# Steps that fill PSUM banks for VectorE go to the front of a cell, and four pairs' first scores are made side by side

## The chip, the cores and the metric

The kernel runs on one core of a Trainium2 chip. The metric is the device time of one execution in microseconds (us). Three runs of the kernel before took 1527.48, 1527.50 and 1529.93 us; the median is 1527.5 us. The core's engines are TensorE (PE: matrix products, results to PSUM), VectorE (DVE), ScalarE (ACT), GpSimd (POOL) and SyncE (SP, which here only issues DMA transfers). PSUM has eight banks of 128 x 512 float32 each; TensorE writes them, VectorE and ScalarE empty them.

## The reference

Two transformer blocks over `x` of 2 sequences x 1024 rows x 256 features, with a context of 2 x 64 rows; everything is float32, with 16 heads of 16 features.

```python
# block 0
q = ln(x);  x = x + mha(q, q)                       # self-attention, 16 heads
x = x + mha(ln(x), ln(ctx))                         # cross-attention over 64 rows
h = ln(x);  logits = h @ router.T                   # 8 experts, the best 2 of each row
x = x + sum over 2 experts of gate * (gelu(h @ fc1.T) @ fc2.T)
# block 1
x = x + self_attention(ln0(x))
x = x + cross_attention(ln1(x), ctx, mask)          # a masked context row gets -10000
x = x + gelu(ln2(x) @ fc1.T + b1) @ fc2.T + b2
```

In each attention `softmax(q k / 4) v` is computed; the largest score of a row is subtracted before the exponential.

## The kernel before

The text calls reference block 0 "block 1" and reference block 1 "block 2", as the change's title does; in the code they are `layer` 0 and 1.

**Cells.** Self-attention of one block is 128 cells in a written-out order (`self_attention`, the loop over `cell`). A cell belongs to one group of four heads, one half of the queries and one 128-key chunk: `h, n = divmod(cell, 8)`. It does two things on TensorE, in four lanes on four row groups (`scores`, L969): "b" tiles, the scores of this cell with keys on the partitions and the row's largest score subtracted, and "a" tiles, the scores of the cell `LEAD` = 10 further on with queries on the partitions. ScalarE empties a "b" bank with an exponential (L947); VectorE empties an "a" bank with a maximum along the row (L937). Every eighth cell `collect(h)` joins the maxima of a group (L1002 to L1004, three VectorE operations; the middle one writes to a PSUM bank out of the free list), and one cell later `largest(h)` transposes them (L835). From cell 118 on there are no "a" tiles.

Exponentials are multiplied with the values in `product` (L1024): either two cells in one PSUM bank, or one cell alone (`alone`) when the cell has little other work. ScalarE copies the result out (L1036), and GpSimd, or VectorE from cell 118 on (`helper()`), adds it up (L1037).

**Other chains in the cells.** Everything else is a `Task`: a generator whose steps give their cost in planned microseconds, or a negative number for a pause. In each cell `Stream.steady(cell, 1.1)` takes one step of each "light" task in order of `rank` while less than 1.1 planned us are spent; `Stream.step` fills odd cells with heavier ones; what is left over decides whether a product is done alone. After the last cell `Stream.rest` runs what remains, by rank and pause. Since the engines' orders are written out this way, each engine executes in exactly the order in which the steps are called.

For each quarter n of the rows, a block has these chains: `cnorm` n (layer norm; statistics L398/L399, roots L381 to L389, centring L412, transposes L424), `asked` n (queries, L1295), `weighed` n (cross-attention weights), `cross` n (division and output projection, L492/L500). Block 1 also has `dispatch` n (rank 70: router, choice of two experts, places, L1568 to L1676, with eight indirect DMA writes from GpSimd), `found` (places of the expert tiles, L1693 to L1802) and the expert slots (`turn` L1926, `first` L1961, `second` L1992). Block 2 ends with the dense layer (`forward`, L2145 and L2157).

**`weighed`** (rank 30) has its own first scores: `scores(g, n, ...)` makes the products of head pairs r = 2n and 2n + 1 of half g (L1337), in block 2 after a product that adds the mask (L1324), and VectorE reduces each bank (L1345). `parts` (L1358/L1359) writes the maxima where `largest` transposes them (L1364); then come `weights` (L1374, L1380, exponential L1385), the products with the values (L1434 and the sums L1444) and the division (L1453, L1459, L1466). In the cells with "a" tiles one step does half of the rows of two pairs; in the later cells and in the rest one step does all rows of two pairs, so four steps make the first scores of a quarter.

PSUM banks are handed out by `bank()` from the front of a list and go back to its end when the step that empties them is written down. A matmul waits for the engine that last emptied its bank.

Of the kernel before, what the change touches and what calls it, by code (L numbers as in the profile page):

```python
# [134 lines left out]
class Task:  # L135

    def __init__(self, steps, cost, first=-99, last=None, mark=None, after=(), rank=0, light=False):
        self.steps, self.left, self.first, self.light = steps, cost, first, light  # L140
        self.soft, self.last = last is None, 9999 if last is None else last
        self.mark, self.after, self.rank = mark, after, rank


class Stream:
# [29 lines left out]
    def steady(self, cell, most):  # L175

        spent = 0.0
        for t in sorted((t for t in self.tasks if t.light), key=lambda t: -t.rank):
            if spent < most and t.first <= cell and self.made.issuperset(t.after):
                spent += max(0.0, self.advance(t, cell) or 0.0)  # L180
        return spent

# [53 lines left out]
def two_blocks(  # L236
# [27 lines left out]
    def bank():  # L264


        i = free.pop(0)
        return i, banks[:, i, :]
# [312 lines left out]
    def self_attention(layer, tail, heads, arrive, extra, when_ready, beside=None):  # L581
# [41 lines left out]
        QB, mx = {}, {}  # L623
# [488 lines left out]
        if layer == 0:  # L1112

            fill_up(-LEAD, 4.0)
            owed = 0.0
            for ahead in range(0, LEAD, 2):
                cell = now[0] = ahead - LEAD
                for n, _ in enumerate(early(ahead)):
                    for go in later.pop(cell + n, []):
                        go()  # L1120
                    if (ahead, n) == (6, 1):
                        collect(0)
                    owed += 1.6
                    while owed > 0.6 and (cost := stream.step(cell)):
                        owed -= cost
                    if (ahead, n) == (8, 0):
                        stream.add(largest(0), 0.75, mark=("QB", 0))
                        stream.until(("QB", 0))
        owed = 0.0
        for cell in range(ncell + 2):  # L1130
            now[0] = cell
            ahead = cell + LEAD
            if ahead < ncell and ahead % 16 == 0:
                need_heads(ahead // 8)
            has_a, has_b = ahead < ncell, cell < ncell
            maxima[0] = has_a
            lanes = []
            for j in range(4):
                tiles = [("b", cell, j)] * has_b + [("a", ahead, j)] * has_a
                lanes.append(tiles[::-1] if j > 1 else tiles)  # L1140
            scores(lanes)
            if ahead % 8 == 7 and has_a:
                h = ahead // 8
                collect(h)
                stream.add(
                    largest(h), 0.75, first=cell + 1, last=cell + 2, mark=("QB", h), rank=99, light=True
                )
            if (cell + 1) % 8 == 0 and cell + 1 < ncell:
                stream.until(("QB", (cell + 1) // 8))
            for go in later.pop(cell, []):  # L1150
                go()
            if cell >= 2 and cell % 2 == 0:
                product([c for c in (cell - 2, cell - 1) if c not in alone])
            if has_a:
                most = 2.2 - stream.steady(cell, 1.1)
                while cell % 2 == 1 and most > 0.9:
                    cost = stream.step(cell, heavy=True)
                    if cost is None:
                        break
                    most -= cost  # L1160
            else:
                owed = min(owed, 3.0) + max(stream.pace(cell), 2.0)
                if cell % 2 == 0 and owed < 2.5:
                    continue
                most = 2.2
                while owed > 0.5 and most > 0.0:
                    cost = stream.step(cell)
                    if cost is None:
                        break
                    owed -= cost  # L1170
                    most -= cost

            if cell % 2 == 1 and most > 1.2 and cell < ncell:
                alone.add(cell - 1)
                product([cell - 1])
# [79 lines left out]
    def cross_tasks(stream, layer, n, pool, first):  # L1255


        att = 2 * layer + 1
        w = weights[att]
        b, t0 = n // 2, 4 * n  # L1260
        name = f"c{layer}{n}"
        held = {}

        def norm():
            xT = held["xT"] = pool.tile([P, 2, 512], F32, tag="cx", name=f"xT_{name}")
            yield from norm_task(t0, 4, "cq" if layer == 0 else "ln1", xT, name)
            if layer == 0:
                add_bias(t0, 4, bias_out[1])

        before = [(m, n - 1) for m in ("cross", "asked")] if n > 0 else ["context"]  # L1270
        stream.add(norm(), 2.0, mark=("cnorm", n), after=before[1:], first=first,
            rank=67 if layer == 0 else 40, light=True)
        stream.add(
            ask(layer, pool, w, name, held), 3.44, mark=("asked", n),
            after=[("cnorm", n), before[0]], rank=30,
        )
        stream.add(
            weigh(layer, b, pool, w, name, held), 13.5,
            mark=("weighed", n), after=[("asked", n)], rank=30, light=True,
        )  # L1280
        stream.add(
            share(w, name, t0, held), 5.0, mark=("cross", n),
            after=[("weighed", n)], rank=50,
        )
# [23 lines left out]
    def weigh(layer, b, pool, w, name, held):  # L1308
# [7 lines left out]
        mx = pool.tile([P, 2, 4, 4, 2], F32, tag="mxc", name=f"mx_{name}")  # L1316
        turned_mx = []

        def scores(g, n, t0=0, nt=4):

            got = [(r, *bank()) for r in (2 * n, 2 * n + 1)]
            for r, _, p in got if layer == 1 else ():
                at = slice(32 * r, 32 * r + 1)
                nc.tensor.matmul(  # L1324
# [146 lines left out]
        if whole:  # L1471
# [2 lines left out]
            cells = [[] for _ in range(22)]  # L1474
            for k in range(8):
                g, n, half = k // 4, k // 2 % 2, k % 2
                cells[k].append((scores, g, n, 2 * half, 2))
                if k % 4 == 3:
                    cells[k].append((parts, g))
            cells[9].append((largest,))  # L1480
# [16 lines left out]
            return  # L1497
        costs = {scores: 1.0 + extra, largest: 0.9, weights: 1.2, undivided: 1.9, division: 0.55}
        rs = range(4)
        for step, *args, wait in (  # L1500
            (scores, 0, 0, None),
            (scores, 0, 1, None),
            (parts, 0, None),
            (scores, 1, 0, None),
            (scores, 1, 1, None),
            (parts, 1, -1.8),
            (largest, -0.8),
            (weights, 0, rs, -1.6),
            (undivided, 0, None),
            (weights, 1, rs, -1.6),  # L1510
            (division, 0, None),
            (undivided, 1, None),
        ):
            step(*args)
            if step in costs:
                yield costs[step]
            if wait:
                yield wait
# [988 lines left out]
```

## Time and profile before

| | |
|---|---|
| median of three runs | 1527.5 us |
| profiled execution, whole | 1523.92 us |
| its span (first to last instruction) | 1522.0 us |
| TensorE busy | 1439.3 us (95%) |
| VectorE busy | 982.7 us (65%) |
| ScalarE busy | 919.9 us (60%) |
| GpSimd busy | 355.3 us (23%) |
| mean granted TensorE clock | 0.986 |
| L937, row maxima on VectorE | 1024 of 683 ns |
| L947, exponentials on ScalarE | 1024 of 603 ns |
| L1345, reductions of the cross scores on VectorE | 96 of 506 ns |
| L1036, copies of products | 145 of 601 ns |
| activation-table loads | 17 |

The cells of block 1 lie between about 65 and 545 us of the span, the rest of block 1 and the expert slots between 545 and 900 us, the cells of block 2 between 900 and 1372 us, and its rest after that. An ordinary cell takes 2.7 us with a product alone and 3.6 us with a pair or with a heavier step. How to read the rows shown further on: a row of waits gives the engine that waited, who released it, the sum, the number and the longest wait; a row of a timeline gives start, duration, engine, line, operation, output and inputs, and in brackets the idle time before it; a row of a stretch gives busy time (and instructions) of PE, PEld (weight loads), DVE, ACT and POOL, the granted clock, the share of the DMA engines and GB/s.

### The profile page before, as it was taken

Reading aid. Unit: us, or ns where it says so; the run is one execution under the profiler, and the core shown is the slowest. Engines: PE = TensorE matmul, PEld = TensorE weight load, DVE = VectorE, ACT = ScalarE, POOL = GpSimd, SP = SyncE. Lnnn points to the kernel's source line nnn. Section 1 sums busy time; section 2 is a strip of 40 time slices with the busy share of each in tenths; the row PEclk is TensorE's granted clock in tenths of the full one; section 3 lists DMA queues with packets and bytes.
Section 4 is the critical chain, followed back from the end, with each engine's and each line's share of the span. In section 5 each row is a group of like instructions: output and inputs, shape, how many; then the busy total and the mean of one; then the engine's idle time right before and its main releaser. Section 6 shows DMA issues by size and latency. Waiting matters only on the chain. (4 is left out here: it accounts for less than half of the span.)

```text
span 1522.0 us, 29849 instructions
## 1 busy us (share of the span) xinstructions
PE 1439.3 (95%) x11172; PEld 830.1 (55%) x11172; DVE 982.7 (65%) x2216; ACT 919.9 (60%) x1797; POOL 355.3 (23%) x488
## 2 busy tenths in 40 slices
PE   6999999999999977999999999999999999999998
PEld 3444444444434445788888664444454454446676
DVE  7867788869778665531115758877886886944210
ACT  3377788777777845323323347877877777783411
POOL 2221234225243122031112023211332322411010
PEclk9899999999999998999999999999999999999999
DMA  8653122111110030666566541132211112000000
GB/s 318 248 217 136 52 70 64 43 47 42 36 51 31 15 115 29 215 240 232 188 203 231 169 150 62 61 108 71 64 50 52 44 36 97 29 10 29 8 14 28
DMA packets 69157, 148.71 MB, mean 98 GB/s; under 512 B 12842, under 2 KB 26668, under 8 KB 68620
## 3 DMA queue, kind: packets, MB, share of 16 engines
q1 hardware_dynamic: 65788, 137.86, 26.6%
q0 software_dynamic: 3216, 8.85, 1.6%
q8 instruction: 91, 1.49, 0.4%
q14 instruction: 62, 0.51, 0.1%
HBM read 94.32 MB, written 51.99 MB: 96 GB/s over the span
## 5 line engine op out<-in xcount | busy, mean ns | idle before, releaser
L937 DVE TENSOR_REDUCE mx_s<-banks 128x1 f32<-128x512 f32 x1024 | 635.4, 683 | 131.2 <-PE banks L969 123.4
L947 ACT ACTIVATE pt_s<-banks 128x512 f32<-128x512 f32 x1024 | 535.2, 603 | 125.9 <-PE banks L969 120.1
L1024 PE MATMUL banks<-pt_s,v_s 128*18 128x512 f32 x2048 | 260.6, 603 | 9.6 <-ACT pt_s L947 5.4
L1037 POOL TENSOR_TENSOR acc_s<-acc_s,part_s 128x512 f32<-128x512 f32 x130 | 166.8, 1283 | 419.5 <-ACT part_s L1036 418.8
L969 PE MATMUL banks<-qb_s,ones 2*128 2x512 f32 x1024 | 200.6, 395 | 0.0
L1992 PE MATMUL banks<-w_slot,h_s 128*128 128x256 f32 x560 | 125.1, 380 | 0.4 <-DVE spread L1004 0.4
L1036 ACT COPY part_s<-banks 128x512 f32<-128x512 f32 x145 | 87.1, 601 | 48.0 <-PE banks L1024 42.6
L1992 PEld LDWEIGHTS banks<-w_slot,h_s 128*128 128x128 f32 x560 | 105.4, 190 | 15.6 <-DVE spread L1004 0.8
L1024 PEld LDWEIGHTS banks<-pt_s,v_s 128*18 128x18 f32 x2048 | 43.5, 97 | 126.8 <-ACT pt_s L947 66.4
L2001 DVE SCALAR_TENSOR_TENSOR ys<-banks,gate,b 128x256 f32<-128x256 f32 x35 | 16.9, 483 | 133.2 <-PE banks L1992 133.2
L969 PEld LDWEIGHTS banks<-qb_s,ones 2*128 2x128 f32 x1024 | 96.6, 186 | 8.9
L1967 ACT ACTIVATE h_s<-banks,w_slot 128x256 f32<-128x256 f32 (+1 forms) x104 | 41.1, 446 | 86.1 <-issue 48.3
L2007 POOL DMA_INDIRECT results<-ys,to x35 | 33.8, 966 | 224.3 <-DVE ys L2001 175.6
L1961 PE MATMUL banks<-xsT,w_slot 128*128 128x256 f32 (+1 forms) x416 | 84.9, 357 | 0.9 <-ACT xsT L431 0.9
L1961 PEld LDWEIGHTS banks<-xsT,w_slot 128*128 128x128 f32 x416 | 70.9, 190 | 12.0 <-issue 2.8
L2145 PE MATMUL banks<-hT_f,w_ff 128*128 128x512 f32 x128 | 57.0, 595 | 0.0
L2157 PE MATMUL banks<-w_ff,h_f 128*128 128x256 f32 x256 | 56.6, 379 | 0.0
L1345 DVE TENSOR_REDUCE mx_c<-banks 128x4 f32<-128x256 f32 (+1 forms) x96 | 44.2, 506 | 17.8 <-PE banks L1337 16.7
L698 PE MATMUL banks<-xT_s,w_att 128*128 128x512 f32 x104 | 50.9, 613 | 3.2 <-ACT pt_s L947 2.4
L1967 ACT ACTIVATE h_s<-banks,spare 128x256 f32<-128x256 f32 (+1 forms) x56 | 21.7, 444 | 51.1 <-PE banks L1961 34.9
L2157 PEld LDWEIGHTS banks<-w_ff,h_f 128*128 128x128 f32 x256 | 48.2, 190 | 7.2 <-issue 1.0
L2148 ACT ACTIVATE h_f<-banks,w_ff 128x512 f32<-128x512 f32 x32 | 21.9, 687 | 48.6 <-PE banks L2145 48.6
(376 smaller groups left out, 2926.8 us busy)
## 6 DMA issues: line engine op xcount, KB each, us to landing
w_slot<-in_ff_w_dram SPq DMA_DIRECT2D x40, 576.0 KB
sorted_rows<-fill SPq DMA_DIRECT2D x36, 520.0 KB
w_slot<-in_ff_w_dram SPq DMA_DIRECT2D x26, 514.0 KB
whole<-acc_s SPq DMA_DIRECT2D x30, 256.0 KB
spare<-in_ff_w_dram SPq DMA_DIRECT2D x14, 514.0 KB
q_parts<-spare SPq DMA_DIRECT2D x13, 512.0 KB
KS<-k_parts SPq DMA_DIRECT2D x12, 512.0 KB
k_parts<-spare SPq DMA_DIRECT2D x10, 512.0 KB
```

Source lines behind the costliest of these rows:

```text
L698: nc.tensor.matmul(p, lhsT=w[:, at + k * D + pair * P : at + k * D + (pair + 1) * P], rhs=xT[b][:, k, blk * 512 : (blk + 1) * 512], start= ...
L937: nc.vector.tensor_reduce(to, sc, AX.X, ALU.max)
L947: nc.scalar.activation(pt, sc, AF.Exp, scale=SCALE)
L969: nc.tensor.matmul(sc, lhsT=lhsT, rhs=rhs, start=now[0] == 1, stop=last)
L1024: nc.tensor.matmul(o[32 * j : 32 * j + VW, :], lhsT=V[b][:, cell % 8, 4 * g + j, :], rhs=exps.pop((cell, j)), start=(cell == cells[0]), st ...
L1036: nc.scalar.copy(part, o)
L1037: helper().tensor_tensor(acc[h], acc[h], part, ALU.add)
L1961: nc.tensor.matmul(ph[:, n, :], lhsT=w[:, at : at + P], rhs=xT[:, k, :], start=(k == 0), stop=(k == 1),)
L1967: nc.scalar.activation(h1[:, f, :rows], ph[:, n, :], AF.Gelu, bias=w[:, W_B1 + f : W_B1 + f + 1])
L1992: nc.tensor.matmul(py, lhsT=h1[:, f, h * P : (h + 1) * P], rhs=w[:, f * D : (f + 1) * D], start=(f == 0), stop=(f == 7),)
L2145: nc.tensor.matmul(ph, lhsT=w1[:, at : at + P], rhs=hT[:, k, :], start=(k == 0), stop=(k == 1))
L2157: nc.tensor.matmul(py[:, n, :], lhsT=h1[:, f, t * P : (t + 1) * P], rhs=w2[:, f * D : (f + 1) * D], start=(f == 0), stop=(f == 7),)
```

## The change

1. A `Task` gets a flag `drains`. The tasks `largest` (QB) and `weighed` have it. In `steady` the tasks with the flag come first whatever their rank, and tasks without it may begin while 1.8 planned us are spent instead of 1.1.
2. `collect(h)` is called after `steady` instead of before it.
3. In block 2's late cells and rest, `scores` takes all four pairs of a half in one step (planned cost 1.7 instead of twice 1.2). Block 1 keeps two pairs a step there.

```diff
-    def __init__(self, steps, cost, first=-99, last=None, mark=None, after=(), rank=0, light=False):
+    def __init__(
+        self, steps, cost, first=-99, last=None, mark=None, after=(), rank=0, light=False, drains=False
+    ):
+        self.drains = drains
...
-        for t in sorted((t for t in self.tasks if t.light), key=lambda t: -t.rank):
-            if spent < most and t.first <= cell and self.made.issuperset(t.after):
+        for t in sorted((t for t in self.tasks if t.light), key=lambda t: (-t.drains, -t.rank)):
+            if spent < most + 0.7 * (not t.drains) and t.first <= cell and self.made.issuperset(t.after):
...
                 h = ahead // 8
-                collect(h)
                 stream.add(
-                    largest(h), 0.75, first=cell + 1, last=cell + 2, mark=("QB", h), rank=99, light=True
+                    largest(h), 0.75, first=cell + 1, last=cell + 2, mark=("QB", h), rank=99,
+                    light=True, drains=True,
                 )
...
                 most = 2.2 - stream.steady(cell, 1.1)
+                if ahead % 8 == 7:
+                    collect(ahead // 8)
...
             weigh(layer, b, pool, w, name, held), 13.5,
-            mark=("weighed", n), after=[("asked", n)], rank=30, light=True,
+            mark=("weighed", n), after=[("asked", n)], rank=30, light=True, drains=True,
...
-        def scores(g, n, t0=0, nt=4):
+        def scores(g, rs, t0=0, nt=4):
 
-            got = [(r, *bank()) for r in (2 * n, 2 * n + 1)]
+            got = [(r, *bank()) for r in rs]
...
-                cells[k].append((scores, g, n, 2 * half, 2))
+                cells[k].append((scores, g, (2 * n, 2 * n + 1), 2 * half, 2))
...
         rs = range(4)
+        if layer == 1:
+            costs[scores] = 1.7
+            halves = [rs]
+        else:
+            halves = [(0, 1), (2, 3)]
         for step, *args, wait in (
-            (scores, 0, 0, None),
-            (scores, 0, 1, None),
+            *((scores, 0, half, None) for half in halves),
             (parts, 0, None),
-            (scores, 1, 0, None),
-            (scores, 1, 1, None),
+            *((scores, 1, half, None) for half in halves),
             (parts, 1, -1.8),
```

In the order of instructions this gives the following. In block 1, TensorE's order is the same up to cell 88 and again from the fourth expert slot's transposes on. In between, the second quarter's `weighed` steps start one cell earlier and stand ahead of the `dispatch` steps of the same cell; `dispatch` of the second quarter begins two cells earlier and has its places by the end of the cells, and its 14 root operations are on GpSimd instead of VectorE. The program has five L1036 copies fewer (more products are done in pairs) and two activation-table loads fewer; all products and all DMA transfers are the same in number. In block 2 TensorE's order is the same up to cell 118; there VectorE's three `collect` operations move back, behind the reductions or statistics of the same cell. From cell 119 to cell 124 the third quarter's `weighed` steps are fewer and come earlier; in the rest only the four score steps of the last quarter become two.

More of the change, by code (lines that the diff above doesn't have):

```diff
@@ L1126, in self_attention @@
                     if (ahead, n) == (8, 0):
-                        stream.add(largest(0), 0.75, mark=("QB", 0))
+                        stream.add(largest(0), 0.75, mark=("QB", 0), drains=True)
                         stream.until(("QB", 0))
```

## The prediction

> **What bounds the kernel now.** Four views carry it, read in this order. First the page: TensorE is busy for most of the span, so a gain has to come out of its waits and out of the slices in which its clock is cut.
>
> ```profile
> span 1522.0 us, 29849 instructions
> PE 1439.3 (95%) x11172; PEld 830.1 (55%) x11172; DVE 982.7 (65%) x2216; ACT 919.9 (60%) x1797; POOL 355.3 (23%) x488
> ```
>
> Second, the waits of TensorE between 390 and 660 us, the only stretch in which its order of work differs much between the two kernels (cell 89 of block 1 to the third expert slot):
>
> ```profile
> PE banks L424 <- DVE xn_c L412: 9.3, 1, 9.3
> PE banks L969 <- DVE mx_c L1345: 3.7, 3, 1.7
> ...
> PE banks L1364 <- DVE spread L1359: 2.3, 1, 2.3
> ```
>
> The second row is what the change is aimed at: scores of a cell (L969) waiting for PSUM banks that VectorE's cross-attention reductions (L1345) empty. Third, busy time by stretch (columns after the width: PE, PEld, DVE, ACT, POOL, granted clock, DMA):
>
> ```profile
> 404.80:427.20 22.40, 17.80 (x178) 9.11 (x176) 21.84 (x54) 13.34 (x26) 6.39 (x5) 0.97 0.11 37
> ...
> 505.80:541.90 36.10, 34.09 (x340) 16.91 (x340) 16.56 (x53) 30.04 (x61) 0.43 (x1) 1.00 0.00 1
> ...
> 563.20:572.60 9.40, 0.05 (x2) 0.05 (x1) 8.20 (x45) 0.84 (x4) 0.00 (x0) 0.63 0.49 192
> ...
> 1242.30:1259.30 17.00, 16.75 (x185) 8.60 (x186) 15.22 (x32) 14.10 (x28) 5.17 (x4) 1.00 0.14 49
> ...
> 425.80:432.60 6.80, 6.80 (x41) 2.44 (x40) 5.31 (x15) 3.94 (x8) 0.00 (x0) 0.50 0.22 72
> ```
>
> VectorE is full in the first row, with TensorE at 17.8 of 22.4 us; TensorE's own waits there come to 4.6 us. Row 4 is the same cells, 93 to 97, in block 2, where no dispatch work is threaded in: they took 17.0 us there, and 24.7 us in block 1 (406.1 to 430.8). The last row is a slice at half clock right behind the full stretch. Fourth, the order of time inside it:
>
> ```profile
> 418.43 1.09 DVE L1609 TENSOR_TENSOR hot_m<-desc,first_m 128x32 f32<-128x32 f32 x1
> 419.44 0.74 DVE L1345 TENSOR_REDUCE mx_c<-banks 128x4 f32<-128x256 f32 x2
> 419.90 0.50 PE L969 MATMUL banks<-QS00h,KS 32*128 32x512 f32 x1 [1.66 <-DVE mx_c L1345]
> ```
>
> The dispatch operations stand ahead of the reduction that frees the bank, and TensorE stops for 1.66 us. One of them takes 1.09 us where its neighbours take 0.19, with a GpSimd addition (1.26 us from 418.20) under way.
>
> **The change part by part.** Costs are against the profiled execution: 1522.0 us of span and 1.9 around it, 1523.9 us in all, 3.6 under the median of 1527.5.
>
> *1. Block 1, cells 89 to 104.* The built order shows weighed.1 (second quarter's cross weights) starting in cell 89, not 90, and keeping that lead; five L1036 copies in all disappear, because more products are done in pairs. One pair of reductions leaves the full stretch for cell 89, where VectorE has room: two at 0.33 us (spacing of the 0.74 us pairs), 0.7 us, certain. Reordering within a full engine gives nothing by itself: 20 score reductions (12.4 us), ten L1345 (3.7 us) and 5.7 us of other work have to be done in any order. The gain above 0.7 lies in what is not full: the wait in cell 89 (0.5 us), and the half clock. In those 6.8 us TensorE lost up to half, 3.4 us. Bounds: a gain of 3.4 if the slice does not come, nothing if it does, a loss of 3.4 if two come; I take a gain of 1.7, half way, since the waits before it get shorter by the one pair but do not go. Sum -2.4 (+2.7 to -5.4, the latter by taking for each of the 16 cells the longer of its TensorE and VectorE work, which leaves 65.6 us where today the same work takes 71.0).
>
> The row says that the clock fell with waits of 1.66 us at the longest. The Trainium skill, "TensorE: Matmul & The Clock Gate", section "What's actually happening", has the clock cut after an idle window of about 3.4 us, which no wait here reaches; by that rule the cut is not of these waits' making, my 1.7 us would be no gain, and the total -3.4.
>
> *2. Block 1, cells 117 to 128.* The ten product steps become six: 4 copies of 0.6 us, 2.4 us off ScalarE, which is at 30.0 of 36.1 us and makes TensorE wait 1.6 us there (L947, L431). I take -1.0, nearer the waits than the copies (-2.4, and on the other side +2.0 by what follows). dispatch.1 comes two cells earlier; its 14 root operations go from VectorE to GpSimd, where the same 14 took 3.9 us (485.2 to 489.1), read three cells later. Cover: three cells of about 3.5 us. If that cover is gone, L1568 on VectorE, and the L1345 reductions queued behind it, wait some 2 us, and TensorE for their banks.
>
> *3. The rest between the blocks.* The longest wait is this one:
>
> ```profile
> 561.48 0.18 DVE L1776 TENSOR_SCALAR row<-row,begin 128x1 f32<-128x1 f32 x1
> ...
> 562.15 0.68 DVE L500 TENSOR_TENSOR x_sb<-x_sb,banks 128x512 f32<-128x512 f32 x1
> ...
> 563.82 0.14 DVE L1799 TENSOR_SCALAR ntu<-ntu 128x16 f32<-128x16 f32 x1
> ...
> 572.56 1.11 PE L424 MATMUL banks<-ident,xn_c 128*128 128x128 f32 x4 [9.35 <-DVE xn_c L412]
> 573.46 1.06 PE L1926 MATMUL banks<-ident,xs 128*128 128x128 f32 x4
> ```
>
> Behind the last projection VectorE adds, measures, takes roots, twice, before TensorE has anything. Eight operations of found.2 (four from 561.48, four from 563.82) sit in that chain; now they precede the last addition: -1.3 us. The L1641/L1642 waits (0.44 and 0.30) leave this stretch: -0.7. The four L1926 transposes now stand ahead of the L424 ones and run inside the wait (their rows' load was issued at 565.4 and DMA is quiet from 569): -0.6; what is queued behind that load's wait is only L424, not ready before. Against it, seven slot.0 operations (2.4 us) now precede xd_m on VectorE; but first matmuls of the slot start 5.9 us after the first L424 today, and the same VectorE work lies before them afterwards. Eight dispatch.1 sends of 1.27 us on GpSimd start some 5 us earlier and delay nothing; SP's list of loads is the same. Two activation-table loads (1.28 us each) fewer on ScalarE, off the path: 0. Sum -2.6; I take -2.0 (+2.4, if the slot's operations are in nobody's shadow, to -4.5, with the half clock that lies from 566 to 576 us cut short).
>
> From the slots on (about 655 us) the orders agree again and TensorE is over 99% busy, so what is gained before arrives at the end.
>
> *4. The three maxima operations moved back in both blocks.* For heads 8, 9, 12, 13 their scratch bank is no longer last in the free list but third last (fifth, once). Nearest row: L969 waiting 0.2 us for L1004. Eight times 0 to 0.2: +0.3 (0 to +1.6).
>
> *5. Block 2's end.* Scores of four pairs in one step:
>
> ```profile
> 1415.79 0.50 PE L1324 MATMUL banks<-mask_f,ones 1*128 1x512 f32 x2
> ...
> 1416.58 0.50 PE L1324 MATMUL banks<-mask_f,ones 1*128 1x512 f32 x2
> ...
> 1422.79 0.19 DVE L1359 TENSOR_TENSOR spread<-mx_c,spread 128x32 f32<-128x32 f32 x1
> 1423.04 0.66 PE L1364 MATMUL banks<-ident,spread 128*128 128x128 f32 x4
> ```
>
> Two pairs cost 0.79 us now, four steps 3.2. Side by side the saving is between 0 and half. In the rest (weighed.3) it is worth nothing: TensorE reaches L1364 as VectorE's eight reductions end, and would wait for what it saves. In cells 119 to 121 the same eight reductions get less cover: from the second step to the transposes lies only one cell's scores (0.8 us) against 0.3 + 4 x 0.6 + 0.4 = 3.1 us, a wait of 2.3 us. Today the corresponding waits are for banks (12.7 us from 1339.6 for some 10.6 us of work, 2.1 lost). Then L1434 comes a cell after the weights, not two, and waits about 1 us; everything is a cell ahead by then. 0 (+3.3 to -2).
>
> Total -2.4 - 1.0 - 2.0 + 0.3 + 0 = -5.1: the profiled execution would take 1518.8 us, the median 1522.4.
>
> **The rivals.** *A, VectorE bound, nothing more:* only 0.7 + 0.8 (parts 1 and 3) come. For it: 21.84 of 22.40 us busy. Against: part 3 is a chain, not throughput. 1526.0. *B, slower:* the wait ahead of L1364 in block 2's cell 121. 2.3 + 1.0 us, and, as the waits above were followed by half clock, a slice of 6.8 us at half: 3.4. +6.7, on top of A's -1.5: 1532.7. It decides once that wait exceeds block 1's gain. Against: bank waits of the same size are there today. *C, both clock slices go:* -5.4 - 1.0 - 4.5 = -10.9, 1516.6. For it: all waits in part 1 lie just before the cut. Against: the cut's phase is not the kernel's.
>
> **How the numbers follow.** Main case 0.50, A 0.19, B 0.18, C 0.13. One measurement of this kernel can tell about 0.2%, 3.1 us, from none: below 1524.4 is faster, above 1530.6 slower. Nine in ten of the main case (0.45) and C (0.13) are faster: 0.58. Most of A (0.17) and some of the main case (0.04) are the same: 0.21. B and the ends of A and of the main case (0.03) are slower: 0.21. The main case's own range is 1518 to 1526. Leaving out the far half of C and what lies beyond B's price gives 1515.5 to 1533.
>
> **What would show it.** Right: L969 waits for L1345 in cells 93 to 97 under 2 us, VectorE still full there but for one cell less; no half clock near 420 to 432; the wait of L424 for xn_c at 8 us or less, with L1926 inside it; block 2 up to cell 118 unchanged within 1 us. Wrong: a new L1364 wait over 3 us in block 2, or part 4's bank waits of more than 0.2 us a head, or a wait of L1568 on GpSimd's roots.

## The result, and the profile after

The changed kernel took 1536.83 us (median; 1534.70 to 1540.53), the kernel before 1527.5 us beside it: a ratio of 1.006, with a 95% interval from 1.0043 to 1.0077. The change costs 9.3 us where the prediction had a gain of 5.1.

The head of the page of the changed kernel:

```profile
span 1534.2 us, 29842 instructions
PE 1442.0 (94%) x11172; PEld 833.0 (54%) x11172; DVE 972.5 (63%) x2199; ACT 916.9 (60%) x1790; POOL 356.8 (23%) x500
```

The work of the five engines is all but the same; the span is 12.2 us longer than in the profile of before (the medians differ by 9.3; a later paragraph says why the two profiles are no clean pair). (Lines moved with the edit: L969 is now L972, L1024 is L1027, L1345 is L1350, L1364 is L1369, L1926 is L1934, L424 is L427, the sends L1676 are L1684.)

The waits of TensorE between 400 and 470 us, the cells 89 to 107 of block 1:

```profile
PE banks L972 <- DVE mx_s L940: 1.4, 1, 1.4
PE banks L1379 <- issue: 1.2, 1, 1.2
...
PE banks L972 <- DVE mx_c L1350: 0.2, 1, 0.2
```

What the change was to remove is gone: scores waiting for the cross reductions fell from 3.7 us to 0.2 (last row). New is a wait for "issue", which means that nothing in the trace explains why TensorE stood still. The same view between 540 and 665 us, the rest between the blocks:

```profile
PE banks L427 <- DVE xn_c L415: 5.6, 1, 5.6
...
PE banks L1934 <- DMA xs<-sorted_rows: 2.3, 1, 2.3
...
PE banks L889 <- issue: 2.2, 4, 1.0
```

The expected order is there too (the L1934 transposes run inside the long wait, which is 5.65 us after them), and again there are stops for "issue", at L889. The order of time around them, with PE, POOL, DVE and ACT rows (the POOL rows are the fifth and the eighth of the eight sends):

```profile
550.07 1.58 PE L1449 MATMUL banks<-pt_c,picks 128*32 128x128 f32 x32
...
551.12 0.97 POOL L1684 DMA_INDIRECT sorted_rows<-xd_m,at_m  x1 [0.17 <-issue]
...
552.26 1.08 PE L883 MATMUL banks<-acc_s,picks 128*64 128x512 f32 x4
...
553.27 0.42 PE L889 MATMUL banks<-acc_s,picks 128*32 128x128 f32 x4
...
554.93 0.96 POOL L1684 DMA_INDIRECT sorted_rows<-xd_m,at_m  x1 [0.30 <-issue]
...
557.14 0.96 DVE L1458 RECIPROCAL inv_c<-banks 128x128 f32<-128x128 f32 x1 [6.62 <-remote]
557.27 0.59 ACT L898 COPY ot_s<-banks 128x512 f32<-128x512 f32 x1 [5.42 <-remote]
```

VectorE's reciprocal needs only the L1449 sums, which TensorE had done at 551.65; ScalarE's copy needs L883, done at 553.34. Both start 1.25 to 1.4 us after GpSimd's last send has ended, within 0.13 us of each other. The trace also keeps the moments at which TensorE raises its semaphore: one at 551.24, the next at 557.12, although four matmuls that raise it had ended from 551.65 on; the four rises then come together, from 557.12 to 557.25. So TensorE's completions reached the others up to 5.5 us late (by the ends that the trace gives for matmuls, which are modelled). Its own matmuls came in small groups meanwhile. TensorE's clock paid a second time (columns: width, PE, PEld, DVE, ACT, POOL, granted clock, DMA share, GB/s):

```profile
551.25:557.15 5.90, 3.39 (x25) 1.35 (x26) 0.01 (x1) 0.59 (x1) 3.73 (x4) 1.00 0.61 224
557.50:567.70 10.20, 8.87 (x34) 8.02 (x35) 5.49 (x25) 2.44 (x6) 0.00 (x0) 0.50 0.00 1
```

VectorE did next to nothing in the first row, and the second is half clock. The same happened at 441 to 448 us, where the sends of dispatch.0 run. Of the ten rises that matmuls ending from 442.03 to 447.35 us call for, the trace has four, so the engines that wait tell it better:

```profile
442.94 0.72 PE L972 MATMUL banks<-KS,QS01l 32*128 32x512 f32 x2
...
447.71 1.29 DVE L940 TENSOR_REDUCE mx_s<-banks 128x1 f32<-128x512 f32 x2 [2.91 <-PE banks L1385]
```

VectorE's third and fourth maximum of the cell need these matmuls, the first of which ended at 443.44. VectorE was free from 444.79 and started at 447.71, 4.3 us after that end; the releaser that the view names, L1385, writes other banks. ScalarE's third exponential started 4.2 us late. Cell 100 takes 8.70 us, and the slice from 444.8 to 455.0 us is at half clock.

Set beside the first profile of before by stretches (cells by the mean start of their four exponentials; us, and differences from before; e-numbers are the experiments below, letters their chips):

| stretch | before | changed | e18: sorting alone, A | e17: maxima alone, A | e9: changed, C | e14: sorting alone, D | e16: before, D |
|---|---|---|---|---|---|---|---|
| to block 1, cell 0 | 65.2 | +0.5 | -1.7 | -1.9 | -1.7 | -2.9 | -1.4 |
| cells 0 to 89 | 325.1 | -0.5 | -0.1 | +1.2 | -1.0 | -0.1 | -1.1 |
| cells 89 to 98 | 40.5 | -2.7 | -2.7 | -1.0 | -3.0 | -4.1 | -2.1 |
| cells 98 to 105 | 28.6 | **+9.1** | **+10.3** | -0.3 | +0.7 | +0.7 | -0.7 |
| cells 105 to 127 | 83.1 | -4.0 | -4.5 | -0.1 | -4.0 | -4.5 | -0.1 |
| rest, to block 2 | 357.2 | **+9.8** | **+7.8** | **+6.5** | -0.4 | -0.4 | +1.2 |
| block 2, 0 to 118 | 435.8 | 0.0 | 0.0 | -0.2 | -0.2 | -1.5 | -0.2 |
| 118 to the end | 186.5 | 0.0 | -0.2 | 0.0 | +1.5 | -0.2 | 0.0 |
| span | 1522.0 | +12.2 | +8.7 | +4.3 | -8.1 | -13.0 | -4.5 |

The whole loss lies in two stretches, and in both GpSimd issues sends. One execution differs from the next by some microseconds (e9 and e14 lie 5.4 and 4.3 us under the medians of their own runs), so the table tells where, and the medians below tell how much.

The two profiles of the first comparison are no clean pair. The profile of before took 1523.9 us, less than each of the five executions that give the median (1526.67 to 1529.93), and it is none of them; it has no late completion and lacks no record of VectorE's semaphore (2051 rises for 2049 instructions), where the profile of the changed kernel lacks 30 (1981 for 2011). The experiments below find the first picture on three chips and the second on one.

### The profile page after: what moved, and what is told of

It reads as the page before. It is cut to its first block, busy times and chain, and to the rows that moved or that the text cites. A ratio compares the mean times of both kernels' runs of the same rounds, so it can differ in the third digit from the quotient of the medians.

```text
span 1534.2 us, 29842 instructions
## 1 busy us (share of the span) xinstructions
PE 1442.0 (94%) x11172; PEld 833.0 (54%) x11172; DVE 972.5 (63%) x2199; ACT 916.9 (60%) x1790; POOL 356.8 (23%) x500
## 5 line engine op out<-in xcount | busy, mean ns | idle before, releaser
L1027 PE MATMUL banks<-pt_s,v_s 128*18 128x512 f32 x2048 | 258.5, 605 | 10.6 <-ACT pt_s L950 5.4
L972 PE MATMUL banks<-qb_s,ones 2*128 2x512 f32 x1024 | 200.5, 395 | 0.0
L1027 PEld LDWEIGHTS banks<-pt_s,v_s 128*18 128x18 f32 x2048 | 43.7, 97 | 130.2 <-ACT pt_s L950 65.3
L1039 ACT COPY part_s<-banks 128x512 f32<-128x512 f32 x140 | 83.9, 599 | 47.4 <-PE banks L1027 43.9
L972 PEld LDWEIGHTS banks<-qb_s,ones 2*128 2x128 f32 x1024 | 96.0, 186 | 8.8
L1975 ACT ACTIVATE h_s<-banks,w_slot 128x256 f32<-128x256 f32 (+1 forms) x104 | 41.1, 446 | 83.1 <-issue 49.2
L1350 DVE TENSOR_REDUCE mx_c<-banks 128x4 f32<-128x256 f32 (+1 forms) x96 | 44.0, 504 | 22.6 <-PE banks L1342 21.3
```

Source lines behind the costliest of these rows:

```text
L972: nc.tensor.matmul(sc, lhsT=lhsT, rhs=rhs, start=now[0] == 1, stop=last)
L1027: nc.tensor.matmul(o[32 * j : 32 * j + VW, :], lhsT=V[b][:, cell % 8, 4 * g + j, :], rhs=exps.pop((cell, j)), start=(cell == cells[0]), st ...
L1039: nc.scalar.copy(part, o)
L1975: nc.scalar.activation(h1[:, f, :rows], ph[:, n, :], AF.Gelu, bias=w[:, W_B1 + f : W_B1 + f + 1])
```

## The experiments

The experiments ran on four chips, here called A (e1 to e4, e17, e18), B (e5 to e8), C (e9 to e12) and D (e13 to e16). Ratios are to the kernel before on the same chip at the same time. Edits are shown by what they come to; in most of these kernels the parts of the change stand behind switches. No profile of the unedited kernel before was taken on A; e2 and e17 have its order in block 1.

| run | kernel | chip | median us | before | ratio, 95% interval | completions late? |
|---|---|---|---|---|---|---|
| e1 | changed | A | 1535.24 | 1526.58 | 1.0047 (1.0032 to 1.0062) | up to 4.7 us |
| e9 | changed | C | 1521.33 | 1521.38 | 1.0004 (0.9992 to 1.0015) | no |
| e13 | changed | D | 1522.95 | 1521.16 | 1.0014 (1.0004 to 1.0023) | no |
| e2 | block 2 only | A | 1529.42 | 1526.58 | 1.0023 (1.0007 to 1.0040) | up to 3.5 |
| e3 | maxima in front | A | 1530.36 | 1526.58 | 1.0020 (1.0010 to 1.0030) | up to 5.4 |
| e4 | no allowance | A | 1532.98 | 1526.58 | 1.0041 (1.0027 to 1.0055) | up to 5.8 |
| e6 | side by side alone | B | 1523.44 | 1521.10 | 1.0016 (1.0004 to 1.0027) | no |
| e17 | maxima moved alone | A | 1530.29 | 1528.02 | 1.0021 (1.0006 to 1.0035) | up to 3.5 |
| e7 | sorting alone | B | 1514.96 | 1521.10 | 0.9958 (0.9941 to 0.9974) | no |
| e10 | sorting alone | C | 1517.38 | 1521.38 | 0.9964 (0.9950 to 0.9979) | no |
| e14 | sorting alone | D | 1515.22 | 1521.16 | 0.9967 (0.9954 to 0.9979) | no |
| e18 | sorting alone | A | 1528.46 | 1528.02 | 1.0010 (0.9995 to 1.0026) | up to 5.8 |
| e8 | sorting, no allowance | B | 1516.24 | 1521.10 | 0.9973 (0.9960 to 0.9986) | no |
| e11 | sorting, no allowance | C | 1514.55 | 1521.38 | 0.9957 (0.9944 to 0.9971) | no |
| e15 | sorting, no allowance | D | 1512.80 | 1521.16 | 0.9951 (0.9936 to 0.9966) | no |
| e5, e12, e16 | before, one execution each | B, C, D | 1522.56, 1523.55, 1519.43 | | | no |

"Late" is the largest distance between the end of a TensorE matmul and the rise of its semaphore inside a gap of over 1.2 us between such rises, taken up to 615 us. In e8 and e10 the records show 1.3 and 1.1 us once, but there rises are missing: in e8 the reciprocal that waits starts at 597.49 us, 0.1 us after its matmul's end. The starts of waiting engines confirm the others: while sends run in the cells, maxima and exponentials begin up to 1.4 us (e2, e4, e17) or 3.6 to 4.3 us (the others) after their matmul's end though the engine is free; in the twelve other profiles never more than 0.9 us. The gaps behind 615 us also fall into sends, and none of the conclusions rests on them. Profiles with late completions, and the chip that has them, are called disturbed, the others clean or undisturbed.

### First on A: which half, which part

e1 is the changed kernel, unedited.

> The changed kernel as it is, profiled a second time. Theory O (the order of block 1 costs the time): cell 100 of block 1 again takes over 8 us, TensorE again stands still for some 4 us while GpSimd sends the rows of dispatch.1 (551 to 557 us in the first profile), each with a half-clock slice behind it, and the span is 1534 us within 3. Theory X (the two stalls belong to that one execution): at least one of them is absent or lies elsewhere, and the span is 5 us or more shorter where it is absent.

The second profile repeats the first: cell 100 takes 8.39 us, completions are late by 4.7 us from 551.45 to 556.58, the rest is 6.8 us longer than before's, the span 1533.9 us. Not the accident of one execution.

e2 keeps block 1 as before. Its edit against the changed kernel:

```diff
+        stream.drain = layer in (1,)
...
-        for t in sorted((t for t in self.tasks if t.light), key=lambda t: (-t.drains, -t.rank)):
-            if spent < most + 0.7 * (not t.drains) and t.first <= cell and self.made.issuperset(t.after):
+        d = self.drain
+        for t in sorted((t for t in self.tasks if t.light), key=lambda t: (-t.drains * d, -t.rank)):
+            if spent < most + 0.7 * d * (not t.drains) and t.first <= cell and self.made.issuperset(t.after):
...
                 h = ahead // 8
+                if layer not in (1,):
+                    collect(h)
...
-                if ahead % 8 == 7:
+                if ahead % 8 == 7 and layer in (1,):
                     collect(ahead // 8)
```

> Block 1 keeps the order of before; block 2 has all of the change (the three maxima operations moved back, and the first scores of four pairs side by side at its end; the sorting of steps changes no order there). Theory O: the loss is all in block 1, so 1527.5 us within 2. Rival S (the side by side scores or the moved maxima cost, hidden in the first comparison by gains elsewhere): 1530 us or more. If block 2's change is a gain by itself, under 1525 us.

It lost 2.8 us, at the edge of theory O's range and just under rival S's. Two things came with it: block 2's change has a price of its own, and completions were late in block 1 although its order is before's (3.5 us, while the projections ran), with the rest 6.4 us longer than in the first profile of before. So late completions come with before's order too.

e3 is the changed kernel with the three maxima operations back in front, in both blocks:

```diff
             if ahead % 8 == 7 and has_a:
                 h = ahead // 8
+                collect(h)
...
-                if ahead % 8 == 7:
-                    collect(ahead // 8)
```

> The changed kernel with the three maxima operations back in front of the cell's steps, in both blocks. Theory O: they cost 0.47 us at cells 45 and 77 of block 1 and some 1.5 us in block 2 by the first comparison, so 1535 us within 2; the stalls near cell 100 and at 551 us stay. Rival M (the moved maxima operations are what pushes block 1's cells apart): 1529 us or less and no stall at cell 100.

4.9 us less than the changed kernel, between the two theories, and the two long stretches stay (cell 100 8.77 us; the rest +7.8). The maxima cost more than expected, but they do not bring the stalls.

e4 leaves out the allowance:

```diff
-            if spent < most + 0.7 * (not t.drains) and t.first <= cell and self.made.issuperset(t.after):
+            if spent < most and t.first <= cell and self.made.issuperset(t.after):
```

> The changed kernel without the 0.7 us that other steps may run over a cell's allowance. Products still come first, but dispatch.0 is spread over more cells: its sends fall in cells 108 to 111 instead of 101 to 104. From cell 119 on the order is that of the changed kernel. If the sends that share cells 100 to 104 with the products make cell 100 long, cell 100 falls to 5.5 us (what its like in block 2 take) and the time to 1533 us within 2; if it is the pair and the product in one cell alone, cell 100 stays above 8 us and the time at 1536.8. In both the stall in the rest between the blocks stays.

Here cell 100 holds the same pair of products and the same product step as in the changed kernel, but no sends. It takes 5.49 us, on the chip where the changed kernel needs 8.4 to 8.8. The sends moved to 466 to 478 us, and the late completions moved along: none in cells 98 to 105, and beside the sends up to 1.4 us (an exponential at 478.07 us whose matmul ended at 476.68). The time came out as expected (1532.98 us). So on this chip the pair and the product alone do not make cell 100 long; it takes the sends beside them. The sends behind cell 127 stayed where they were, and so did the lateness there (5.8 us, rest +6.4).

### On B: parts alone

> The kernel before, profiled a second time. In the five profiles of kernels that hold any part of the change, TensorE's completions reach the other engines 1 to 6 us late while GpSimd issues its sends (indirect DMAs), and in the first profile of the kernel before none is late. Theory L (the sends delay completions in every kernel and the first profile of before was a lucky execution): gaps of 2 to 4 us in TensorE's completions during the sends here too, and a span above 1524 us. Theory O (before's order of steps keeps the sends clear of it): no such gap, span 1522 to 1524 us.

No gap in the kernel before; the span, 1520.6 us, is under what either theory had, since B is faster than the first comparison. e6 is before with its last edit only:

```diff
-        for step, *args, wait in (
-            (scores, 0, 0, None),
-            (scores, 0, 1, None),
+        halves = [rs] if layer == 1 else [(0, 1), (2, 3)]
+        if layer == 1:
+            costs[scores] = 1.7
+        for step, *args, wait in (
+            *((scores, 0, half, None) for half in halves),
```

(and the same for `scores, 1`).

> The kernel before with the scores of four pairs side by side at block 2's end as its only edit. By the prediction's part 5: no difference (0, between +3.3 and -2 us). By the four other profiles that have it: the end is 1.5 to 2.8 us longer, because a half-clock slice of 3.4 to 6.8 us (1.4 us lost for each 3.4) comes near 1350 us, so 1528.3 us within 1.5. If there is no such slice, 1526.6.

2.4 us by the ratio (0.6 to 4.1), although the profiled execution has no slice of half clock at the end and shows nothing but a different arrangement of the same 40 us. Other executions have less clock: the mean granted clock is 0.9848 in e6's twelve and 0.9864 in before's 24. That difference is some 5 us of half clock an execution, and at the 1.4 to 1.5 us for each 3.4 us that the other profiles show, an estimate of 2 us. e7 is the sorting and the allowance alone, e8 the sorting without the allowance:

```diff
-        for t in sorted((t for t in self.tasks if t.light), key=lambda t: -t.rank):
-            if spent < most and t.first <= cell and self.made.issuperset(t.after):
+        for t in sorted((t for t in self.tasks if t.light), key=lambda t: (-t.drains, -t.rank)):
+            if spent < most + 0.7 * (not t.drains) and t.first <= cell and self.made.issuperset(t.after):
```

> The kernel before with the sorting by drains and the 0.7 us over the allowance as its only edit: maxima operations in front, scores at block 2's end by two pairs. It changes the order in block 1 alone. From the profile with the maxima in front: cells 89 to 127 gain 0.8 us; the rest between the blocks loses 5 us by late completions that the last normalization (VectorE's reciprocal, ScalarE's copy behind the last sums) waits for. Expected 1529.5 us, within 1.5, and again a gap of over 5 us in TensorE's completions behind cell 127. If side by side scores and sorting only cost together, 1526.6 or less.

> The same without the 0.7 us over the allowance, so that dispatch.0's sends fall in cells 108 to 111. Cells 89 to 127 gained 2.2 us with the moved maxima operations in (0.55 of which they cost), so 2.7 us here; the rest loses 5 us. Expected 1528 us within 1.5: 1.5 to 2 us under the sorting with the allowance. If the sends' place in the cells does not matter, no difference between the two.

Both expectations fell, in the good direction: 6.4 and 4.1 us faster than before, and not one late completion behind cell 127. The same order that had stalled on A (e3) ran clean here. Either the chip decides, or the sorting needs one of the other parts to stall.

### On C and D: the same kernels again

> The changed kernel a third time, on one chip with the next three. So far late completions during the sends were in all profiles of the first two calls' chips but not in one of the third call's. Theory C (the chip decides): all four profiles of this call have them, or none has. With them this kernel is 8 to 10 us over before; without them 1 to 4 us under it (sorting alone -6.1, the moved maxima operations +2, the side by side scores 0.7 to 2.3). Theory K (the kernel decides: two of the change's parts together bring them): this kernel has them and is 8 to 10 us over before, whatever the next two show.

> Sorting alone a second time. Theory C: if the late completions are there, it loses in the rest between the blocks and is 2 us over before, within 2; if not, 6 us under before, as on the other chip. Theory K: no late completions, 6 us under before.

> Sorting alone without the allowance, a second time. Theory C: with late completions 0 to 2 us over before, since its sends in the cells meet fewer products; without them 5 us under before. Theory K: none, 5 us under before.

> The kernel before, a third profile, on the chip of the three others. Theory C: it has late completions during its sends if the others have, and then its rest between the blocks is 3 to 6 us longer than 357 us, as in the profile with block 2 alone changed. Theory K: none.

The changed kernel itself runs clean on C, with the time of before (1 to 4 us less had been expected). That excludes theory K. The order of time of the same instructions as above:

```profile
538.78 0.95 PE L1449 MATMUL banks<-pt_c,picks 128*32 128x128 f32 x28
...
539.79 0.96 DVE L1458 RECIPROCAL inv_c<-banks 128x128 f32<-128x128 f32 x1 [0.68 <-PE banks L1449]
539.97 1.08 PE L883 MATMUL banks<-acc_s,picks 128*64 128x512 f32 x4
...
540.98 0.96 POOL L1684 DMA_INDIRECT sorted_rows<-xd_m,at_m  x1 [0.30 <-issue]
540.98 0.65 PE L889 MATMUL banks<-acc_s,picks 128*32 128x128 f32 x16
...
541.12 0.59 ACT L898 COPY ot_s<-banks 128x512 f32<-128x512 f32 x1 [1.54 <-PE banks L883]
```

The view begins inside the L1449 sums, so its first row has 28 of the 32. The sends run beside the same matmuls, and the reciprocal starts 0.1 us after the sums. The window that answers to 551.25 to 557.15 (both begin 0.13 us into the first send behind `vbd`'s memset and last 5.9 us):

```profile
539.85:545.75 5.90, 4.43 (x42) 3.00 (x42) 4.26 (x18) 1.17 (x2) 3.70 (x4) 1.00 0.60 216
```

DMA moves as much (216 against 224 GB/s) and GpSimd works as long (3.70 against 3.73 us), but VectorE has 4.26 us of work done instead of 0.01.

> The changed kernel a fourth time. Theory C (the chip decides): with late completions in the profile 6 to 10 us over before; without them within 1.5 us of before.

> Sorting alone. With late completions on this chip: 9 us over the clean value, so 2 to 4 us over before (the gap of over 5 us behind cell 127 and the long cell 100 come from the sorted order); without them 4 to 6 us under before. If sorting alone has no late completions where the changed kernel has them, it is not the chip but the other two parts that bring them.

> Sorting alone without the allowance. With late completions: 0 to 3 us over before (only the gap behind cell 127 is left); without them 5 to 7 us under before.

> The kernel before, a fourth profile. If the chip decides and this one is of the first kind: late completions of 1 to 4 us during its sends and 1 to 6 us more in the rest between the blocks. If the chip is of the second kind, or the kernel decides: none.

D is clean as well. The changed kernel is 1.8 us over before, a little more than expected. Cell 100 takes 5.48 to 5.51 us in all eight clean profiles with sorted order, with or without sends in it (e9 has five), and 8.39 to 8.77 us in the four with late completions that have sends in it (the first changed profile, e1, e3, e18).

### A once more

e17 is before with the maxima operations moved, and nothing else:

```diff
             if ahead % 8 == 7 and has_a:
                 h = ahead // 8
-                collect(h)
...
+                if ahead % 8 == 7:
+                    collect(ahead // 8)
```

> The kernel before with the three maxima operations moved behind the cell's steps in both blocks, as its only edit. The prediction had +0.3 us (0 to 1.6) for it. By the stretches that hold the heads (0.5 us each at cells 45 and 77 of block 1, 1.2 us in block 2's cells 60 to 118): 2.2 us over before, within 1. If all of what the changed kernel loses against its sorting alone came from it: 5 to 7 us over before.

> Sorting alone a fourth time. Without late completions 4 to 6 us under before, as on three chips; with them 2 to 4 us over before if the chip decides, still under before if the late completions need the other two parts.

e17 gives 3.2 us by the ratio (0.9 to 5.3), at the upper edge of what was expected. The waits of TensorE in cell 45, in the first profile of before and then in e17 (whose L974 and L1009 are before's L969 and L1004):

```profile
PE banks L969 <- DVE spread L1004: 0.2, 1, 0.2
```

```profile
PE banks L974 <- DVE spread L1009: 1.1, 1, 1.1
```

The operations come 0.9 us later, TensorE waits for the bank they write, and the cell gets 0.46 us longer. Cell 77 of block 1 and cells 77 and 109 of block 2 do the same, four heads of eight.

e18 answers the main question: it is the place of the run and not the two other parts. On A the sorting alone loses its gain: 1528.46 us, where it took 1515 to 1517 on the other three (against before 1.5 us more by the ratio, between -0.8 and +4.0; 2 to 4 had been expected). Its waits behind cell 127 and its order of time:

```profile
PE banks L1468 <- DVE count L1701: 3.5, 1, 3.5
```

```profile
548.85 1.06 PE L1453 MATMUL banks<-pt_c,picks 128*32 128x128 f32 x32
...
553.69 0.96 POOL L1684 DMA_INDIRECT sorted_rows<-xd_m,at_m  x1 [0.30 <-issue]
555.75 0.96 DVE L1462 RECIPROCAL inv_c<-banks 128x128 f32<-128x128 f32 x1 [6.46 <-remote]
```

TensorE is held up little here, the reciprocal all the same 5.8 us. So the delay is in the news of a completion, not only in the matmuls.

In e17 the order is before's, and the sends meet the projections instead of the closing sums. The profile of before shows that order:

```profile
548.39 0.96 DVE L1453 RECIPROCAL inv_c<-banks 128x128 f32<-128x128 f32 x1 [0.46 <-PE banks L1444]
...
549.89 1.08 POOL L1676 DMA_INDIRECT sorted_rows<-xd_m,at_m  x1 [4.39 <-DVE at_m L1668]
...
554.41 1.89 PE L492 MATMUL banks<-w_att,q_c 128*128 128x256 f32 x8
```

The first send of dispatch.1 starts after the reciprocal, and the projections (L492) run among the later ones. In e17 this wait follows:

```profile
PE banks L428 <- DVE xn_c L416: 11.5, 1, 11.5
```

Late completions make the long wait 2.2 us longer there (9.35 in the first profile of before), and do nothing to cells 98 to 105 (-0.3 us).

The prices by medians, disturbed chip against the three others: before 1526.6 and 1528.0 against 1521.1 to 1521.4, 5.2 to 6.9 us; sorting alone 1528.5 against 1515.0 to 1517.4, 11.1 to 13.5 us; the changed kernel 1535.2 against 1521.3 and 1523.0, 12.3 to 13.9 us. The sorted order pays twice as much; by the table the difference lies where its sends share cells 98 to 105 with products and where they meet the sums at the end of attention.

The parts add up. On A: sorting +0.0010, maxima +0.0021, side by side +0.0016 (from B) give 1.0047, and e1 measured 1.0047. On undisturbed chips: sorting -0.0037 (mean of three) with the same two gives 1.0000; measured 1.0004 and 1.0014. Each ratio is known to about 0.0015, so that the sums agree as well as this is partly luck.

Not tried: taking the sends away, because later loads read the rows that they write. So it is shown that the late completions go with the sends (they move with them, and every gap with a completion over 1 us late has at least one send in it), not that sends alone suffice; on B, C and D they do not. What sets A apart stays open: it was measured twice with B, C and D in between, so the time of the run is not it, but the chip itself, the machine around it or other work beside it are not told apart. The chip of the first comparison was not noted; its profile of the changed kernel looks like A's, and before's median there (1527.5) too.

On B, C and D two kernels beat both: the sorting alone (0.9958 to 0.9967) and the sorting alone without the allowance (0.9951 to 0.9973). On A the latter was only run with the two other parts (e4, 1.0041, where the changed kernel has 1.0047).

## Why the prediction was wrong, point by point

**The step that failed** is in part 3: "Eight dispatch.1 sends of 1.27 us on GpSimd start some 5 us earlier and delay nothing." In the first comparison's profile TensorE's completions come up to 5.5 us late beside them, and starting earlier puts them beside the last sums instead of beside the projections: rest +9.8 us where -2.0 was predicted. On undisturbed chips they do delay nothing (e9: the reciprocal starts 0.1 us after its sums). Part 1 did not price dispatch.0's sends at all, which the change leaves in cells 99 to 102 while it moves products in beside them: +9.1 us. The first profile of before could not show it: it has no late completion.

That the changed kernel took 1521.3 and 1523.0 us on C and D, close to the predicted 1522.4, is luck: before took 1521 there too, and no gain was measured.

**Part 1**, -2.4, holds where completions are on time. The wait of scores for L1345 fell from 3.7 to 0.2 us, under the 2 us that were asked for. Cells 89 to 117, sorting alone against before on the same chip: -0.9, -3.5, -2.0 us (B, C, D). The half-clock slice near 412 to 432 us mostly stayed (seven of the eight clean sorted profiles have 3.4 us or more of it, e15 none), so the 1.7 us for its loss came only in part. The far bound of -5.4 starts from 71.0 us for these cells; by the table above they took 69.1.

**Part 2**, -1.0, was too small: cells 117 to 127 are 3.1 us shorter in every sorted profile, of which 0.7 us is work that now lies behind cell 127 (the closing sums start 0.7 us later after it). The roots on GpSimd held nobody up.

**Part 3**, -2.0, is -0.4 to -0.6 on undisturbed chips in the profiles of e7, e9, e13 and e14, or -1.1 if the 0.7 us that part 2 pushed in are taken off. Four other clean profiles have the same order there: e10, e11 and e15, with a half-clock slice more, are at +2.0, +1.4 and +1.6, and e8 at -2.2. So its size is known to some 2 us only. From the last projection's end to the transposes of xn_c it is 8.8 us (e9) after 9.35: 0.56 us from the chain, not 1.3. The four slot transposes stand inside the wait as predicted, but now themselves wait for their rows (3.8 us), which costs nothing as xn_c comes later still.

**Part 4**, +0.3, is 1.85 us: 0.46 in four cells. The indicator was named, "bank waits of more than 0.2 us a head": 1.1 us. The prediction looked at the heads whose place in the free list changes (8, 9, 12 and 13). The cells that got longer belong to others, h = 6 and 10 in block 1 and 10 and 14 in block 2 of `collect(h)`: there VectorE comes to the operations 0.9 us later, and TensorE waits for the bank within the same cell.

**Part 5**, 0: the wait ahead of L1364 was priced at 2.3 us and is 2.6, and the scores saved pay for it, as said. What was left out of the likeliest case is the clock. Six of the eight profiles with side by side scores have a slice of half clock near cell 121 of block 2, one of twelve without. In e9 the wait and the slice are:

```profile
1338.88 0.92 PE L1369 MATMUL banks<-ident,spread 128*128 128x128 f32 x4 [2.58 <-DVE spread L1364]
```

```profile
1339.10:1342.50 3.40, 3.40 (x24) 2.15 (x26) 1.97 (x4) 1.80 (x4) 2.64 (x2) 0.51 0.00 0
```

Each 3.4 us of it costs 1.4 to 1.5 us at the end. That is rival B's mechanism at half of its clock price (3.4 us for a slice of 6.8, where most here are 3.4 long); it is real, but not what decided.

With the sizes as measured, the sum on undisturbed chips is -2.1 - 2.4 - 1.1 + 1.85 + 1.5, about -2 us; measured 0 (C) and +2 (D, between +0.6 and +3.5). So even without late completions the predicted gain did not come, by parts 4 and 5; the late completions turned that into a clear loss.

## What to carry to other kernels

Before moving a chain of indirect sends, or moving work beside one, ask who waits for completions while they run, and price a delay of some microseconds, even if the profile at hand shows none: one profile is one chip. Measure the parts of a change alone; here one part gained 4 to 6 us and two small ones gave it all back. And a change that is to be kept is better tried on several chips, since here a gain of 4 to 6 us on three chips was none on the fourth.

## What the runs showed of the hardware

- On one chip of four, in all six profiles, TensorE's completions were up to 3.5 to 5.8 us late while GpSimd issued indirect DMAs; in twelve profiles on three other chips none was found over 1 us late. For VectorE and ScalarE lateness is not shown: after a VectorE operation that ends at 443.98 us in the first changed profile the next rise on record comes 4.4 us later, but the rises of two operations are missing there.
- The disturbed profiles also lack event records: VectorE raised its semaphore 2004 times by e18's trace, where its instructions call for 2032; e7's trace, of the same kernel, has 2030. In all six profiles on A 27 to 38 are missing, in the twelve on the other chips 2 at most. Whether recording has a part in the delay can't be told from these runs.
- Half clock begins within microseconds of waits shorter than its slice: in e9 at 1339.10 us, 0.2 us after a wait of 2.6 us. TensorE was busy for 0.83 us of the 3.41 us before. The Trainium skill, "TensorE: Matmul & The Clock Gate", "What's actually happening", has windows of 3413 ns that run freely, with the clock cut after an idle one. The lengths agree (3.4, 6.8, 10.2, 13.7 and 17.1 us occur); read as idle throughout, the rule does not, and the measurement decides.
